# Attention with a spectral branch on one core: two diagonal row tiles share score columns, and the first loads, fills and projections are placed anew

## The chip, the cores and the metric

The kernel runs on one NeuronCore of a Trainium2 chip. The metric is the device time of one execution in microseconds (us), taken as the median of several executions. A profile of one execution shows every instruction of the five engines: TensorE (PE; its weight loads are shown apart as PEld), VectorE (DVE), ScalarE (ACT), GpSimd (POOL) and SyncE (SP, which here only issues DMAs).

## What is computed

The input x is 2 x 2048 x 256 (B = 2, S = 2048, D = 256). Cut to what matters, the reference is:

```
xn = layernorm(x)
q, k, v = xn @ wq, xn @ wk, xn @ wv      # 16 query heads, 4 key/value heads of 16
q, k = rope(q), rope(k)
scores = q k^T / 4, causal               # -inf above the diagonal
attn = softmax(scores) v
out = x + attn @ wo + real(ifft(fft(xn) @ w)) + bias
```

The spectral branch is linear, so the kernel turns its weights into one 256 x 256 matrix and multiplies with it.

## The kernel before, in words

**Tiles and stages.** The rows are cut into 8 blocks of 512 (`SB`), in the order (batch 0, j = 0), (batch 1, j = 0), (batch 0, j = 1) and so on, with j from 0 to 3. A block is 4 row tiles of 128 (`NI`). The 16 query heads are 4 groups of 4 heads, so there are 32 units (n, g) of a block and a group. All products of scores are made of bf16 parts: q and k are split in three parts each and stacked on 112 partitions (`qst`, `kst`), which gives scores of nearly float32 quality in one bf16 product. Most products are issued as four matmuls of 32 output partitions each (`product`, L151, with the matmul on L155), one for each quarter of the output partitions.

**Row maxima (kind A).** The softmax needs each row's maximum ahead of the exponentials. `maxima` (L593) makes slots for a unit: `row_max(i, k, pr)` handles row tile i of the block, key block k and two heads. PE writes both heads' scores into a pair of PSUM banks (`sm`, a ring of two such pairs) and DVE reduces them to one maximum for each row and head (L636, into `mx`). Where k is below j all 512 keys count. On the diagonal (k = j) row tile i sees (i + 1) x 128 keys, and each head takes eight matmuls: in each quarter q a mask product that writes -1e30 above the diagonal (L627, from column `at` to the end of the tile) and the scores added to it (L631). The lines are quoted here:

```python
for q in range(0, P, QD):
    to, at = ps[0][q : q + QD, e, :], wd - P + q
    nc.tensor.matmul(to[:, at:wd], ident_h[:, q : q + QD], mask[:, q:],
        start=True, stop=True, skip_group_check=True)
    nc.tensor.matmul(to[:, : at + QD], rows[:, q : q + QD], keys[:, : at + QD],
        start=False, stop=True, skip_group_check=True)
```

After the last slot of a unit `parts` (L644) combines the maxima over the key blocks and splits the negated maximum in three bf16 parts with seven small DVE reductions (L656); `spread` (L668) turns them onto partitions with four PE transposes, an ACT copy (`mt`) and a small DMA into `qst`, so that the next product subtracts the maximum by itself.

**Scores and values (kinds B and V).** `scores` (L693) makes the transposed scores of 128 keys for one head (`st`, three PSUM banks), and ACT takes the exponential (L745, or L747 two heads at once when no A is left). `values` (L767) multiplies them with V (L782). Groups are divided by their sums with DMAs and POOL, and `output` (L920) adds the output projection, the spectral product and x.

**Preparing a block.** `load_x` (L166) loads 512 rows with one DMA on SP. `row_stats`, `row_power` and `row_shift` (L233 to L252) make mean and inverse deviation on DVE and POOL. `project` (L379) normalizes (`norm`, L398), transposes (`transpose_x`, L405), multiplies with the weights (`features`, L419), rotates and splits. Block 0 does this on DVE, all later ones on POOL. `rotary_table` (L276) spreads the cosines and sines over columns (`expand`, eight DVE reductions, L293) and transposes them (`turn`). `ones` (L370) fills `va` and `kst` with ones. At the start PE runs 48 transposes of no use (L997) while the first loads are under way.

**The order.** A planner at the end of the kernel (L1127 on) writes the order of all instructions by hand. It keeps a clock for each engine from estimated costs (`use`, `send`, `through_bank`), takes at each step the piece that could start soonest, and looks up by when each A slot is due (`due`, L969 to L983, built from the `cols` that a slot states). The engines then work through this fixed order; changed costs or slot sizes move pieces everywhere.

Of the kernel before, what the change touches and what calls it, by code (L numbers as in the profile page):

```python
# [17 lines left out]
P = 128  # L18
# [5 lines left out]
def tile_attn_plus_spectral_ffn(  # L24
# [141 lines left out]
    def load_x(n):  # L166
        send("sp", 512, [slot("xt")], [("xt", "in", n)])
        take_slot("xt")
        xt[n] = work.tile([P, NI, D], F32, tag="xt", bufs=2, name=f"xt{n}")
        nc.sync.dma_start(out=xt[n], in_=block_rows(n))  # L170
# [41 lines left out]

    spec = {}
# [3 lines left out]
    def load_late():  # L217

        for name, src, tag, bufs in (
            ("wre", w_re, "inv", 2), ("dc", dft[0], "inv", 2),  # L220
            ("wim", w_im, "attT", 2), ("ds", dft[1], "avs", 3),
        ):
            take_slot(tag)
            spec[name] = work.tile([P, NK, D], F32, tag=tag, bufs=bufs, name=name)
            nc.gpsimd.dma_start(out=spec[name], in_=src.rearrange("(c p) n -> p c n", p=P))
            send("pool", 256, (), ["spec"])
        nc.gpsimd.dma_start(out=wo_sb, in_=wo.rearrange("(c p) n -> p c n", p=P))
        nc.gpsimd.dma_start(out=bias_sb, in_=bias.partition_broadcast(P))

# [3 lines left out]
    def row_stats(n, i):  # L233
        if i == 0:
            mv[n] = work.tile([P, NI, 2], F32, tag="mv", bufs=2, name=f"mv{n}")
        st = work.tile([P, 6], F32, tag="bn", bufs=3, name=f"bn{n}_{i}")
        nc.vector.bn_stats(st, xt[n][:, i, :])
        nc.vector.bn_aggr(mv[n][:, i, :], st)
        use("dve", 0.53, [("xt", "in", n)], [("mv", n)])

    def row_power(n):
        rstd[n] = work.tile([P, NI], F32, tag="rs", bufs=2, name=f"rs{n}")
        nc.gpsimd.tensor_scalar(rstd[n], mv[n][:, :, 1], EPS, None, ALU.add)
        nc.gpsimd.tensor_tensor(rstd[n], rstd[n], neg_half, ALU.pow)
        use("pool", 1.35, [("mv", n)], [("rs", n)])
# [30 lines left out]
    def rotary_table(j):  # L276
        ex = []

        def expand():
# [17 lines left out]
            use("dve", 1.15, at, [("trx", j)])  # L297
# [72 lines left out]
    def ones(n):  # L370
        e, eng, us = (nc.vector, "dve", 2.7) if n == 0 else (nc.gpsimd, "pool", 2.5)
        va[n] = const.tile([P, NI, NKV, QD], F32, tag=f"va{n}", name=f"va{n}")
        e.memset(va[n], 1.0)
        kst[n] = const.tile([P, NKV, SB], BF16, tag=f"kst{n}", name=f"kst{n}")
        for h in range(NKV):
            e.memset(kst[n][96:P, h, :], 1.0)
        use(eng, us, (), [("ones", n)])

    def project(n):  # L379
# [4 lines left out]
        MULT, SUB, CAST, NORM = (0.72, 0.72, 0.46, 0.33) if n == 0 else (1.23, 1.13, 0.63, 0.53)  # L384
        raw, sw, swp, part, ra, at = {}, {}, {}, {}, {}, {}
# [33 lines left out]
        def features(c):  # L419
            ps = bank(f"ps_q{n}_{c}")  # L420
            for k in range(NK):
                product(
                    ps, wp[:, k, c, :], xnT[n][:, k, :], start=(k == 0), stop=(k == NK - 1)
                )
# [3 lines left out]
            through_bank(  # L428
                1.83, ["wp", *(("xnT", n, k) for k in range(NK))], "act", 0.48, [("raw", "in", n, c)],
                [("raw", at[c] - ring["raw"])],  # L430
# [138 lines left out]
        for c in (NK, 0, 1):  # L569
            table = [("cs", j, 1)] * (n >= 2)  # L570
            pe.append(("pe", ["wp", *table, *xs], ["st", "raw"] + ["sw"] * (n >= 2), lambda c=c: features(c)))
# [21 lines left out]
    def maxima(n, g):  # L593
# [3 lines left out]

        def row_max(i, k, pr):

            wd = SB if k < j else (i + 1) * P  # L600
            ps, k_s = [], []

            def head(e):
                if e == 0:
                    k_s.append(take_slot("s"))
                    if not slots_done:
                        t["mx"] = work.tile(
                            [P, NI, NKV, NJ], F32, tag="mx", bufs=3, name=f"mx{n}_{g}"
                        )
                    slots_done.append(1)  # L610
                    ps.append(
                        ps_s.tile([P, 2, SB], F32, tag="s", name=f"sm{n}_{g}_{i}_{k}_{pr}")
                    )
                h = 2 * pr + e
                rows = qst[n, g][0:KC, h, i * P : (i + 1) * P]
                keys = kst[at_block[b, k]][0:KC, h, :]
                use(
                    "pe", (wd + 32 * (k == j)) * 4.28e-4 + (0.012 if k == j else 0.003),
                    [("stk", n, g), ("kst", at_block[b, k]), ("s", k_s[0] - ring["s"])],
                    [("pair", k_s[0])],  # L620
                )
                if k < j:
                    product(ps[0][:, e, :], rows, keys, True, True)
                else:
                    for q in range(0, P, QD):
                        to, at = ps[0][q : q + QD, e, :], wd - P + q
                        nc.tensor.matmul(  # L627
                            to[:, at:wd], ident_h[:, q : q + QD], mask[:, q:],
                            start=True, stop=True, skip_group_check=True,
                        )  # L630
                        nc.tensor.matmul(  # L631
                            to[:, : at + QD], rows[:, q : q + QD], keys[:, : at + QD],
                            start=False, stop=True, skip_group_check=True,
                        )
                if e == 1:
                    nc.vector.tensor_reduce(  # L636
                        t["mx"][:, i, 2 * pr : 2 * pr + 2, k], ps[0][:, :, :wd], AX.X, ALU.max
                    )
                    use("dve", 0.07 + 2 * wd / 960, [("pair", k_s[0])], [("s", k_s[0])])

            needs = [("stk", n, g), ("kst", at_block[b, k])]
            return lambda: head(0), lambda: head(1), 2 * wd + 150, needs

        def parts():  # L644

            top = t["mx"][:, :, :, : j + 1]
# [19 lines left out]
            use("dve", 1.35, (), [("np", n, g)])  # L666

        def spread():  # L668
            ps = bank(f"ps_m{n}_{g}", BF16)
            for i in range(NI):  # L670
                nc.tensor.transpose(
                    ps[0 : 3 * NKV, i * P : (i + 1) * P],
                    t["np"][:, i, :, :].rearrange("p a h -> p (a h)"),
                    ident_h,
# [7 lines left out]
        for i in range(NI):  # L682
            for k in range(j + 1):
                for pr in range(NKV // 2):
                    slots.append(row_max(i, k, pr))
# [170 lines left out]
    def divide(u):  # L856
# [3 lines left out]
        if g == 2:  # L860
            att[n] = work.tile([P, NI, 2, NKV, DH], F32, tag="att", bufs=1, name=f"att{n}")
# [142 lines left out]
    load_late()  # L1004
    row_shift(0)
    order_weights()

    def chain(n, starts, late=0):
# [3 lines left out]
        stats = [("dve", [("xt", "in", n)], [], lambda i=i: row_stats(n, i)) for i in range(NI)]  # L1012
# [5 lines left out]
        if n:  # L1018
            stream([("pool", [], [], lambda: ones(n))], s["ones"], s["stats"])
# [13 lines left out]
    def table(j, since):  # L1033
        expand, turn = rotary_table(j)
        last = [("cs used", at_block[B - 1, j - 2])] if j >= 2 else []
        stream(
            [("dve", last, ["raw", "raw2"], expand)]
# [248 lines left out]
```

## Time and profile before

| what | value |
|---|---|
| median of 3 runs | 926.1 us (925.84 to 926.69) |
| the profiled execution's own time | 926.6 us |
| its span in the profile | 924.9 us |
| mean granted PE clock | 0.995 |
| PE busy | 904.8 us (98%) |
| DVE busy | 749.3 us (81%) |
| ACT busy | 654.3 us (71%) |
| POOL busy | 370.2 us (40%) |

A busy PE counts each matmul from its start to a modelled end. Matmuls of different quarters and following matmuls overlap, so the busy time has the pipeline's latency in it, and idle time under the latency of one matmul is not seen; how fast PE really works is read from the distance between the starts of like groups. "issue" marks idle time that ended without any wait that the profile shows. The span is the time between first and last instruction; 1.7 us of the execution lie around it.

### The profile page before, as it was taken

To read this page: it belongs to the slowest core of one execution; us is meant where nothing else is said; L and a number is where in the kernel's file an instruction comes from. 1 tells how busy PE (TensorE), PEld (TensorE's weight loads), DVE (VectorE), ACT (ScalarE), POOL (GpSimd) and SP (SyncE) were. 2 spreads that over 40 slices of the span, in tenths; PEclk is the share of its full clock that TensorE was granted. 3 is DMA by queue.
4 is the path that set the end of the run, shared out by engine and by line. 5 is a ranking of instruction groups with operands and counts; after the bars stand their busy time and mean duration, and the time that the engine had idled before them with its cause. 6 is when DMAs were issued, how large, how long until landed. Compare 5 with 4: busy or idle time off the path is not lost.

```text
span 924.9 us, 39006 instructions
## 1 busy us (share of the span) xinstructions
PE 904.8 (98%) x17324; PEld 499.3 (54%) x17324; DVE 749.3 (81%) x1062; ACT 654.3 (71%) x1381; POOL 370.2 (40%) x556
## 2 busy tenths in 40 slices
PE   7999899999999999999999999999999999999997
PEld 4655565655555555555555555555455554645443
DVE  6878697789779997898995999979789989788601
ACT  3266665588757784888865777858687878588785
POOL 7287666824672414822246520311571021102121
PEclk9999999999999999999999999999999999999999
DMA  5435724351244011440002510010133001100000
GB/s 162 122 88 139 201 84 115 89 141 39 60 117 133 27 38 31 115 128 26 15 27 85 140 38 14 27 60 14 28 107 93 15 3 38 48 15 14 28 1 24
DMA packets 42024, 62.13 MB, mean 67 GB/s; under 512 B 8872, under 2 KB 32152, under 8 KB 41856
## 3 DMA queue, kind: packets, MB, share of 16 engines
q1 hardware_dynamic: 32432, 41.18, 16.7%
q0 software_dynamic: 8128, 17.69, 5.9%
q8 instruction: 135, 2.21, 1.0%
q10 hardware_dynamic: 1296, 0.79, 0.3%
q14 instruction: 33, 0.27, 0.1%
HBM read 32.75 MB, written 18.40 MB: 55 GB/s over the span
## 4 chain that ended last, share of the span: by engine, by line
PE 89%; DVE 4%; ACT 3%; issue 1%; DMA 1%; SPq 1%; POOL 1%; ACTq 0%; DVEq 0%; POOLq 0%
PE av L782 24%; PE st L155 22%; PE sm L155 17%; PE sm L631 7%; PE po L155 6%; PE ps_q L155 4%; DVE mx L636 2%; PE sp L155 2%; PE sm L627 2%; PE st L738 1%; ACT es L745 1%; PE ps_x L411 1%; PE st L734 1%; ACT es L747 1%; SPq L393 1%
## 5 line engine op out<-in xcount | busy, mean ns | idle before, releaser
L636 DVE TENSOR_REDUCE mx<-sm 128x2 f32<-128x1024 f32 (+3 forms) x640 | 649.1, 1058 | 87.7 <-PE sm L631 45.0
L745 ACT ACTIVATE es<-st 128x512 f32<-128x512 f32 (+3 forms) x1194 | 552.4, 543 | 179.7 <-PE st L155 145.5
L155 PE MATMUL st<-qst,kst 115*32 115x512 bf16 (+3 forms) x4264 | 327.1, 354 | 1.1 <-ACT es L745 0.4
L782 PE MATMUL av<-es,va 128*32 128x512 f32 (+3 forms) x2560 | 299.3, 530 | 0.8 <-issue 0.5
L155 PE MATMUL sm<-kst,qst 112*32 112x512 bf16 x3072 | 239.1, 379 | 0.1
L155 PEld LDWEIGHTS <-kst 115*32 115x32 bf16 x4608 | 160.8, 95 | 140.0 <-issue 64.1
L752 POOL TENSOR_SCALAR_AFFINE_SELECT es<-es 128x256 f32<-128x256 f32 x192 | 76.7, 407 | 274.9 <-ACT es L745 233.4
L155 PEld LDWEIGHTS <-qst 112*32 112x32 bf16 x3072 | 96.0, 96 | 93.0 <-issue 65.0
L631 PE MATMUL sm<-kst,qst 112*32 112x32 bf16 (+15 forms) x2048 | 122.0, 280 | 0.8 <-DMA qst<-part 0.8
L627 PE MATMUL sm<-mask,ident_h 128*32 128x64 bf16 (+3 forms) x2048 | 100.0, 201 | 1.2 <-DVE mx L636 0.9
L782 PEld LDWEIGHTS av<-es,va 128*32 128x32 f32 x2560 | 84.7, 109 | 28.3 <-ACT avs L796 2.6
L631 PEld LDWEIGHTS <-qst 112*32 112x32 bf16 x2048 | 66.1, 97 | 34.3 <-issue 20.7
L627 PEld LDWEIGHTS <-ident_h 128*32 128x32 bf16 x2048 | 66.0, 96 | 32.9 <-issue 26.0
L931 DVE TENSOR_TENSOR xr<-po,xr 128x256 f32<-128x256 f32 x36 | 15.3, 424 | 52.3 <-PE po L155 50.4
L817 POOL DMA_DIRECT2D res<-avs x30 | 18.2, 606 | 81.9 <-ACT avs L796 79.3
L155 PE MATMUL ps_q<-xnT,wp 128*32 128x512 f32 x384 | 45.5, 602 | 0.0
L747 ACT ACTIVATE es<-sp 128x1024 f32<-128x1024 f32 (+3 forms) x43 | 36.5, 907 | 7.3 <-PE sp L155 7.2
L427 ACT COPY raw<-ps_q 128x512 f32<-128x512 f32 x24 | 14.1, 586 | 35.1 <-PE ps_q L155 33.9
L518 POOL TENSOR_TENSOR ra<-raw,cs 128x512 f32<-128x512 f32 (+1 forms) x21 | 27.5, 1307 | 24.2 <-ACT raw L427 23.0
L738 PE MATMUL st<-qst,kst 115*32 115x160 bf16 (+15 forms) x512 | 36.4, 281 | 0.4 <-issue 0.4
L155 PE MATMUL po<-wo_sb,attT 128*32 128x256 f32 x512 | 35.0, 380 | 0.7 <-ACT attT L892 0.7
L734 PE MATMUL st<-mask_t,ident_h 128*32 128x128 bf16 (+3 forms) x512 | 30.6, 202 | 4.2 <-issue 3.3
(113 smaller groups left out, 663.0 us busy)
## 6 DMA issues: line engine op xcount, KB each, us to landing
qst<-run SPq DMA_DIRECT2D x62, 128.0 KB
res<-avs POOLq DMA_DIRECT2D x30, 256.0 KB, 2.9
run<-part SPq DMA_DIRECT2D x31, 192.0 KB
qst<-run SPq DMA_DIRECT2D x31, 192.0 KB
xt<-in_L_attn_x_dram SPq DMA_DIRECT2D x8, 512.0 KB
xr<-in_L_attn_x_dram SPq DMA_DIRECT2D x16, 256.0 KB
sw<-raw SPq DMA_DIRECT2D x60, 64.0 KB
attT<-res POOLq DMA_DIRECT2D x15, 256.0 KB, 4.2
```

The lines of the kernel that those rows point to most:

```text
L155: nc.tensor.matmul(to[q : q + QD], lhsT[:, q : q + QD], rhs, start=start, stop=stop)
L518: e.tensor_tensor(ra[c][:r], raw[c][:r], cs[j][:r, 0, :], ALU.mult)
L627: nc.tensor.matmul(to[:, at:wd], ident_h[:, q : q + QD], mask[:, q:], start=True, stop=True, skip_group_check=True,)
L631: nc.tensor.matmul(to[:, : at + QD], rows[:, q : q + QD], keys[:, : at + QD], start=False, stop=True, skip_group_check=True,)
L636: nc.vector.tensor_reduce(t["mx"][:, i, 2 * pr : 2 * pr + 2, k], ps[0][:, :, :wd], AX.X, ALU.max)
L734: nc.tensor.matmul(to[:, lo : at + QD], ident_h[:, q : q + QD], mask_t[:, : q + QD], start=True, stop=True, skip_group_check=True,)
L738: nc.tensor.matmul(to[:, at:], keys[:, q : q + QD], rows[:, at:], start=False, stop=True, skip_group_check=True,)
L745: nc.scalar.activation(es[u, t, pr][:, e, lo:], ps[:, lo:], AF.Exp, scale=SCALE)
L747: nc.scalar.activation(es[u, t, pr][:, :, lo:], wide[pr][:, :, lo:], AF.Exp, scale=SCALE)
L752: nc.gpsimd.affine_select(out=es[u, t, pr][:, :, lo : lo + P], in_=es[u, t, pr][:, :, lo : lo + P], pattern=[[0, 2], [1, P]], compare_op=A ...
L782: nc.tensor.matmul(av[u][QD * h : QD * (h + 1), lo:], va[at_block[b, t // NI]][:, t % NI, h, :], es[u, t, h // 2][:, h % 2, lo:], start=(t ...
L817: nc.gpsimd.dma_start(out=res[n, c][f], in_=avs[u])
```

## The change

Six things change together.

1. On the diagonal, row tiles 0 and 1 share the columns of one PSUM bank for each head (`first_rows`: 288 columns, two slots for a unit), and tiles 2 and 3 share 800 columns over two banks (`last_rows`: one slot for each head, four for a unit). In the odd tiles the four quarters of rows are taken in turned order, so that quarter q of the one tile needs as many columns more as quarter q of the other needs fewer. Mask products shrink to the 32 x 32 triangle on the diagonal.
2. DVE reduces these slots in groups of 32 columns into a table `top_g`. `parts` has three more small reductions: two add a constant table, which is zero or -1e30 by the row's quarter, to the groups whose owner depends on the quarter, and one takes the maximum over the groups of each tile.
3. `spread` uses matmuls in place of transposes, with a turned identity (`turned_h`) for the odd tiles.
4. The first block of x is loaded with four DMAs, and its statistics wait for their own quarter only. `turned_h` and `top_g` are filled at the start, on DVE and POOL.
5. The spreading of the first table stands between the first block's `row_power` and `row_shift`. The fills of block 1 wait for its normalization.
6. `features` is two pieces for the planner, one for each half of the contraction. Several planner costs are changed, and a late tile takes another buffer's place.

```diff
 def load_x(n):
...
+        step = NI if n else 1
+        for i in range(0, NI, step):
+            nc.sync.dma_start(out=xt[n][:, i : i + step, :], in_=block_rows(n)[:, i : i + step, :])
...
+    turned_h = const.tile([P, P], BF16, name="turned_h")
+    for q in range(0, P, QD):
+        nc.vector.tensor_copy(turned_h[:, q : q + QD], ident_h[:, P - QD - q : P - q])
...
+    G0, TE, TO, STEP = 10, 7, 35, 19
+    top_g = const.tile([P, 2, NKV, 3 * STEP], F32, name="top_g")
+    nc.vector.memset(top_g, NEG)
+    nc.vector.memset(top_g[:, :, :, 0:3], 0.0)
+    nc.vector.memset(top_g[:, :, :, 38:41], 0.0)
...
+        def rows_of(h, i, q):
+            at = i * P + (q if i % 2 == 0 else P - QD - q)
+            return qst[n, g][0:KC, h, at : at + QD]
...
+        def triangle(to, q, first):
+            add(to, ident_h[:, q : q + QD], mask[:, q : q + QD], first)
...
+        def first_rows(pr):
...
+                to = t["ps"][:, e, :]
+                for q in range(0, P, QD):
+                    triangle(to[q : q + QD, q : q + QD], q, True)
+                for q in range(0, P, QD):
+                    triangle(to[q : q + QD, 256:288], q, False)
+                for q in range(0, P, QD):
+                    add(to[q : q + QD, : q + QD], rows_of(h, 0, q), keys(h, 0, q + QD))
+                for q in range(0, P, QD):
+                    add(to[q : q + QD, q + QD : 288], rows_of(h, 1, q), keys(h, 0, 256 - q))
...
+        def last_rows(h):
...
+                    to = t["ps"][:, 1, :]
+                    for q in range(0, P, QD):
+                        triangle(to[q : q + QD, 384:416], q, True)
+                    for q in range(0, P, QD):
+                        add(to[q : q + QD, 0:416], rows_of(h, 3, q), keys(h, P - QD - q, SB - q))
...
+                to = t["ps"][:, 0, :]
+                for q in range(0, P, QD):
+                    triangle(to[q : q + QD, 384 + q : 416 + q], q, True)
+                for q in range(0, P, QD):
+                    add(to[q : q + QD, 128 : 416 + q], rows_of(h, 2, q), keys(h, 0, 288 + q))
+                for q in range(0, P - QD, QD):
+                    add(to[q : q + QD, 416 + q : SB], rows_of(h, 3, q), keys(h, 0, P - QD - q))
...
         def parts():
...
+            for lo, to in ((0, TE), (STEP, TO)):
+                both = rows[:, :, lo : lo + 2 * STEP].rearrange("p r (b c) -> p r c b", b=2)
+                nc.vector.tensor_reduce(rows[:, :, to : to + 3], both[:, :, 0:3, :], AX.X, ALU.add)
+            nc.vector.tensor_reduce(
+                t["mx"][:, :, :, :, j].rearrange("p e r h -> p e (r h)"),
+                rows[:, :, 3 : 3 + 2 * STEP].rearrange("p r (e c) -> p e r c", e=2)[:, :, :, 0:16],
+                AX.X, ALU.max,
+            )
...
     row_power(0)
     load_late()
+    table_0 = rotary_table(0)
+    table_0[0]()
     row_shift(0)
...
-            stream([("pool", [], [], lambda: ones(n))], s["ones"], s["stats"])
+            norm_1 = [("xn", 1, NI - 1)]
+            stream([("pool", norm_1, [], lambda: ones(n))], s["ones"], s["stats"])
```

## The prediction

> **What bounds the kernel now.** I read the page's busy times, then the chain of waits, then windows of stages, then the starts of single groups.
>
> ```profile
> PE 904.8 (98%) x17324; PEld 499.3 (54%) x17324; DVE 749.3 (81%) x1062; ACT 654.3 (71%) x1381; POOL 370.2 (40%) x556
> PE 89%; DVE 4%; ACT 3%; issue 1%; DMA 1%; SPq 1%; POOL 1%; ACTq 0%; DVEq 0%; POOLq 0%
> ```
>
> PE sets the time: it is on 89% of the chain. PE work taken off shortens the run wherever PE itself is full. The windows say where that is:
>
> ```profile
> 80.00:100.00 20.00, 18.54 (x616) 12.01 (x607) 15.80 (x33) 13.58 (x37) 14.54 (x17) 1.00 0.60 157
> 100.00:120.00 20.00, 16.16 (x507) 11.51 (x506) 13.94 (x29) 12.04 (x34) 15.33 (x23) 0.91 0.75 195
> 400.00:500.00 100.00, 99.84 (x1820) 53.53 (x1815) 83.16 (x116) 72.96 (x156) 29.63 (x50) 1.00 0.17 52
> ```
>
> The columns after the stretch and its length are PE, PEld, DVE, ACT, POOL, clock. From 400 to 500 us PE never stops and DVE has 17% to spare. From 80 to 120 us (end of the j = 0 units) no engine is full: they wait for each other. So a PE saving counts fully for the 24 units with j > 0, and in part for the 8 with j = 0.
>
> **Part 1: the diagonal products on PE.** What does such a head cost PE today? The distance of the starts says it. Tile 0 (160 columns in each quarter, 128 of them in the first mask), then tile 3 (544):
>
> ```profile
> 161.09 0.22 PE L627 MATMUL sm<-mask,ident_h 128*32 128x128 bf16 x4
> 161.14 0.22 PE L631 MATMUL sm<-kst,qst 112*32 112x96 bf16 x4
> 161.18 0.22 PE L627 MATMUL sm<-mask,ident_h 128*32 128x128 bf16 x4
> 161.22 0.22 PE L631 MATMUL sm<-kst,qst 112*32 112x96 bf16 x4
> 161.26 0.40 PE L155 MATMUL st<-qst,kst 115*32 115x512 bf16 x4
> ...
> 179.26 0.22 PE L627 MATMUL sm<-mask,ident_h 128*32 128x128 bf16 x4
> 179.31 0.38 PE L631 MATMUL sm<-kst,qst 112*32 112x480 bf16 x4
> 179.50 0.22 PE L627 MATMUL sm<-mask,ident_h 128*32 128x128 bf16 x4
> 179.54 0.39 PE L631 MATMUL sm<-kst,qst 112*32 112x480 bf16 x4
> 179.74 0.41 PE L155 MATMUL st<-qst,kst 115*32 115x512 bf16 x4
> ```
>
> The 0.22 us are latency. The pitch of a head is (161.26 - 161.09) / 2 = 85 ns for tile 0 and 240 ns for tile 3; the same reading gives 125 ns for tile 1 (167.16 to 167.41) and 185 ns for tile 2 (173.63 to 174.00). Sum for a head: 635 ns. Two heads of plain 512-column products take 0.43 us (702.05 to 702.48), which is 0.42 ns a column. By that the four tiles' columns alone would take 67, 121, 175 and 228 ns: each head has 4 to 18 ns more, about 5 ns for each of the two matmuls in a quarter, and most where one has only 32 columns. In tile 0's first quarter 128 columns take 54 + 5 ns, so its 32-column matmul takes the other 26 to 29 ns, not the 13 of its columns.
>
> The change removes, for each head, 1408 - (352 + 448 + 416) = 192 columns in each quarter, and adds 3 matmuls (35 for 32) of which many have 32 columns: two masks in each quarter of `first_rows`, one in each piece of `last_rows`. Two prices:
> - By columns: 192 x 0.42 = 81 ns a head, less the extra matmuls' 5 ns: 10 us for 128 heads of 32 units. The trace's 32-column pitch contradicts it.
> - The Trainium skill ("TensorE: Matmul & The Clock Gate", section "Wait — 56ns, not 53.3ns?") says that start-to-start never drops below about 25 ns however few the columns. This rule speaks against the change, which trades long masks for short ones. The trace has 28 ns by my reading. With 28 ns for each 32-column matmul and 0.42 ns a column + 5 ns otherwise, `first_rows` takes 180 to 196 ns by quarter (mean 187), `last_rows` 206 and 199: 592 ns. Before, by the same formula: 638, which the 635 measured confirm.
>
> I take 46 ns a head, times 128: **-5.9 us**. Ends: -3 (the slowest quarter of each group counts, 611 ns) and -10 (columns). Some 1.5 us of it lies in the j = 0 units, where it counts in part; I leave it in, since the early stage has gains below that I price low.
>
> **Part 2: DVE.** The forms of L636 give its price:
>
> ```profile
> L636 DVE TENSOR_REDUCE mx<-sm 128x2 f32<-128x1024 f32 x448 | 526.6, 1218 | 56.8 <-PE sm L155 35.8 <-PE sm L631 17.6 <-PE st L155 0.6
> L636 DVE TENSOR_REDUCE mx<-sm 128x2 f32<-128x256 f32 x64 | 25.9, 419 | 10.2 <-PE sm L631 9.1
> ```
>
> The slope is (1218 - 419) / 768 = 1.04 ns an element, on 153 ns. Diagonal slots before: 2 x (419 + 685 + 952 + 1218) = 6.55 us a unit. After: two of 576 elements (752 ns) and four of 800 (985 ns), 5.44 us, and in `parts` two reductions of 48 elements (near L656's 170 to 190 ns) and one of 256 (about 420): 0.8 us. Together -0.3 us a unit, 10 us over the run, on an engine with spare time: I cost it at nothing. The 0.8 us also makes the maximum's chain longer (`parts`, `spread`, `mt`, first scores). What hides it is the planner's lead of 3 to 5 score steps of about 1.8 us each; without cover it costs 0.8 x 32 = 25 us, so a lead that fails in a few units costs 1 to 3 us. `spread`'s matmuls have the transposes' columns and stay at L671's price.
>
> **Part 3: the start.**
>
> ```profile
> 5.19 0.43 DVE L237 BATCH_NORM_STATS2 bn<-xt 128x6 f32<-128x256 f32 x1 [0.56 <-DMA xt<-in_L_attn_x_dram]
> ...
> 8.93 0.16 DVE L249 SCALAR_TENSOR_TENSOR sh<-mv,rs 128x4 f32<-128x4 f32 x1 [1.51 <-POOL rs L244]
> 9.01 1.63 DVE L293 TENSOR_REDUCE trx<-trig 128x128 f32<-128x128 f32 x8
> ...
> 10.55 1.89 DVE L399 TENSOR_SCALAR xt<-xt,rs,sh 128x256 f32<-128x256 f32 x4
> ```
>
> DVE waits 0.56 us for x. The quarter loads remove that wait, but the new fills stand ahead of the statistics: four casts of 32 columns (0.4 to 0.6 us, by L208's two 64-column copies in 0.29), 456 elements of `top_g` (0.43, by `va`'s 512 in 0.48), two small fills (0.2): 1.1 us. So the statistics start at about 5.75 and end at 7.95, 0.5 later than now; the split load gains nothing. Then the table (1.63 us) fills DVE's 1.51 us wait for POOL, and the normalization starts at 9.8 in place of 10.55: **-0.75 us**. SP's three more issues (0.5 us each) push the table's load and block 1's back 1.5 us; the table's must land by 7.95, and the first loads are all over by about 8: up to +0.5. POOL's two selections on `top_g` lie in its idle time before 7.5.
>
> PE's useless transposes end at 8.66 and its next work starts at 10.30; in 12 to 15 us the clock is at 0.50. With the gap 1 us shorter the dip may go: between 0 and -1.2 us, I take -0.4.
>
> On POOL's timeline block 1's `rs` (L243) starts only at 18.47, behind the fills of blocks 1 and 2, and later POOL idles: 11.1 us before the next `rs` (33.84), 5.4 us before `ra` (44.87), then it runs without a gap from 48.7 to 80.7. After the change block 1's `rs` follows POOL's six DMA issues, its transposes stand on PE ahead of the spectral products, and POOL can begin its rotation near 27 us in place of 45. PE has no less to do by that; it only starves less at 80 to 120 us. Between 0 and -6 us, near 0 since those windows' waits are mutual: **-2 us**. The split of `features` adds no instruction; where A slots go in between it holds one of three banks longer, 0 to +3 us, I take 0. The late tile's new place was last read near 31 us and is written near 886: nothing.
>
> **Sum:** -5.9 - 0.75 - 0.4 - 2 = -9 us, on the profiled execution's 926.6 (924.9 of span and 1.7 around it): 917.6. The median shown is 0.5 lower: **917 us**.
>
> **Rivals.**
> 1. *The early stage closes up* (17%). 80 to 120 us has 5.3 us without any PE work and 1.7 us lost to a half clock. If the earlier rotation removes that, another 5 us go: 912. Against it: ACT and DVE also stand at 60 to 79% there.
> 2. *The price of short matmuls eats the gain* (14%). Only 24 units count, at 24 ns: -2.3, and -0.75 at the start: 923. For it: 384 more matmul and load pairs.
> 3. *Late instructions, and slower* (11%).
>
> ```profile
> 108.00 0.28 PE L734 MATMUL st<-mask_t,ident_h 128*32 128x128 bf16 x4 [2.92 <-issue]
> ```
>
> PE's program comes in 135 packets of 2.21 MB (the page's q8). The one for this place started only at 105.2, while the DMA engines were full, and PE stood for 2.92 us and then ran 3.4 us at half clock: 4.6 us in all. The Trainium skill ("Runtime: NRT & Kernel Launch", section "Instruction fetch mechanics") holds that fetching in 16 KiB blocks is hidden, which would cost the change's 768 more instructions nothing; this row says otherwise when DMAs crowd. Denser short instructions and transfers moved forward into 50 to 100 us could make such stalls frequent. Two more of them eat the gain, three give 931: slower. Against it: one in 135 today; and today's may vanish as well.
> 4. *As forecast* (58%).
>
> **Range and chances.** Part 1's ends (3 to 10 us), the early stage (0 to 8) and rival 2 give 911.5 to 924, which leaves out rival 3 and the best of rival 1. A measurement tells 0.2% (1.9 us) from no change. Rivals 1 and 4 and most of 2 are faster: 0.85; 0.05 within; 0.10 slower.
>
> **What would show it.** The pitch of a `first_rows` head near 187 ns and of a `last_rows` head near 405; DVE's reductions at 752 and 985 ns; the first normalization near 9.8 us; POOL's first rotation near 27; no new rows of 2 us and more with "issue" on PE. Wrong would be: pitches as before, `mt` later than its unit's first score, or several such stalls.

## The result, and the profile after

The changed kernel takes 920.33 us (median of 12 runs, 918.32 to 923.77); the kernel before took 925.41 us beside it (12 runs, 922.52 to 930.26). The ratio is 0.9951, with a 95% interval of 0.9936 to 0.9966: faster by 0.49%, about 4.5 us (the medians are 5.1 apart). The forecast of 917 us stood for a ratio of 0.990. The sign was right and the time lies in the range, but the gain is about half of the sum of -9 us, and the interval excludes that sum. The profiled execution took 919.05 us, with a span of 917.3 us.

The page of the changed kernel, the same rows as before (busy times, then the packets and megabytes that brought PE's instructions, then the chain of waits):

```profile
PE 891.7 (97%) x17708; PEld 485.7 (53%) x17708; DVE 742.6 (81%) x1101; ACT 655.9 (72%) x1378; POOL 373.0 (41%) x558
...
q8 instruction: 138, 2.26, 1.0%
...
PE 89%; DVE 4%; ACT 4%; issue 3%; ACTq 0%; POOL 0%; DMA 0%; SPq 0%; POOLq 0%; DVEq 0%
```

PE still sets the time. What is new on the chain is "issue": 3% where it was 1%, while DMA and SP's queue have left it. The program needs three more packets of instructions. The windows of the stages (stretch, length, PE, PEld, DVE, ACT, POOL, clock, DMA share, GB/s; the last row is of a second profile of the same kernel, taken with run 10 below):

```profile
80.00:100.00 20.00, 15.39 (x597) 11.11 (x586) 15.24 (x34) 13.70 (x36) 14.02 (x17) 1.00 0.55 152
100.00:120.00 20.00, 17.01 (x594) 12.62 (x598) 16.01 (x34) 13.85 (x36) 12.95 (x20) 1.00 0.60 163
400.00:500.00 100.00, 100.00 (x1889) 53.14 (x1884) 84.76 (x121) 73.38 (x156) 29.91 (x51) 1.00 0.11 35
```

```profile
95.00:100.00 5.00, 4.89 (x151) 3.55 (x154) 2.84 (x4) 2.27 (x7) 2.51 (x4) 0.66 0.52 150
```

From 400 to 500 us PE has no idle time at all, so there the saved PE work counts in full. From 80 to 100 us PE is busy for 15.39 us where it was for 18.54, with about as many matmuls begun (597 for 616): the end of the j = 0 units still starves PE. In this profile the clock is not the reason, since the half clock of before (0.91 from 100 to 120 us) is gone. It is not gone for good: the second profile has 3.4 us of it from 95.5 us on (0.66 over the window of 5 us).

**The diagonal.** PE's timeline around one slot of `last_rows` (start, duration, line, tiles):

```profile
309.66 0.63 PE L155 MATMUL st<-qst,kst 115*32 115x512 bf16 x5
310.11 0.20 PE L677 MATMUL sd<-mask,ident_h 128*32 128x32 bf16 x4
310.14 0.36 PE L677 MATMUL sd<-kst,qst 112*32 112x416 bf16 x4
310.32 0.20 PE L677 MATMUL sd<-mask,ident_h 128*32 128x32 bf16 x4
310.34 0.34 PE L677 MATMUL sd<-kst,qst 112*32 112x288 bf16 x6
310.51 0.38 PE L155 MATMUL st<-qst,kst 115*32 115x512 bf16 x1
```

From 310.11 to 310.51 a head takes 400 ns (forecast 405: 206 and 199), and a group of four 32-column masks, one for each quarter, takes 30 ns of it (310.11 to 310.14). Two heads of `first_rows` start 180 ns apart (100.65 and 100.83; forecast 187). So a head costs 580 to 590 ns in place of 635. DVE's groups by form (busy us, mean ns):

```profile
L652 DVE TENSOR_REDUCE top_g<-sd 128x25 f32<-128x800 f32 x128 | 121.0, 983 | 32.1 <-PE sd L677 27.0 <-PE st L855 3.4 <-PE st L155 0.7
L652 DVE TENSOR_REDUCE top_g<-sd 128x18 f32<-128x576 f32 x64 | 46.8, 749 | 9.9 <-PE sd L677 9.7
L754 DVE TENSOR_REDUCE mx<-top_g 128x16 f32<-128x256 f32 x32 | 13.5, 423 | 1.1
L753 DVE TENSOR_REDUCE top_g<-top_g 128x24 f32<-128x48 f32 x64 | 10.7, 209 | 1.1
```

Forecast were 985, 752, about 420 and 170 to 190 ns.

**The start.** DVE's timeline:

```profile
5.73 0.43 DVE L264 BATCH_NORM_STATS2 bn<-xt 128x6 f32<-128x256 f32 x1
...
7.88 1.60 DVE L320 TENSOR_REDUCE trx<-trig 128x128 f32<-128x128 f32 x8
9.47 0.16 DVE L276 SCALAR_TENSOR_TENSOR sh<-mv,rs 128x4 f32<-128x4 f32 x1
9.67 1.58 DVE L426 TENSOR_SCALAR xt<-xt,rs,sh 128x256 f32<-128x256 f32 x4
```

The statistics start at 5.73 (forecast 5.75), the table fills the wait for POOL, the normalization comes at 9.67 (forecast 9.8, before 10.55). PE's first projection starts at 12.31 in place of 13.76, the half clock of 12 to 15 us is gone, and POOL rotates block 1 from 26.97 (forecast near 27).

**What is new.** The longest entries of PE's waits that ended for no reason that the profile shows (us in total, times, longest):

```profile
PE sd L677 <- issue: 4.7, 4, 1.8
PE st L855 <- issue: 3.4, 3, 1.3
...
PE av L899 <- issue: 1.5, 1, 1.5
```

Before, the same view had 3.3 us on the score masks (two, one of them the 2.92 us row of the prediction) and 0.9 us besides: 4.2 us in all, against 9.6 here. Two of the new ones in the timeline, inside `sd` slots of the j = 0 units, and the longest one of the second profile:

```profile
95.48 0.19 PE L677 MATMUL sd<-mask,ident_h 128*32 128x32 bf16 x2 [1.81 <-issue]
...
100.03 0.20 PE L677 MATMUL sd<-mask,ident_h 128*32 128x32 bf16 x3 [1.49 <-issue]
```

```profile
95.11 0.19 PE L677 MATMUL sd<-mask,ident_h 128*32 128x32 bf16 x2 [2.91 <-issue]
```

PE stops in the middle of a group of four masks, which nothing in the program asks for; a pause of PE is called a stand below. I laid every gap of PE longer than 0.2 us against the 16 KiB packets of the instruction queue, and call a packet "beside" a gap when it is under way in it or ended less than 0.5 us before it. In this profile six gaps of 1.0 us and more have one; the packet starts 1.1 to 1.6 us before PE stands, and PE goes on about 1.4 us after the packet has ended. From 35 to 135 us the gaps with a packet sum to 2.9 us before and to 8.3 us after; in the second profile they sum to 6.2 us, of which 1.2 ended on a wait for ACT. That is rival 3's mechanism: six stands of 1.0 to 1.8 us in this profile in place of one of 2.9, and one of 2.9 us with a half clock behind it in the second.

### The profile page after: what moved, and what is told of

It is laid out like the page before. It is cut to its first block, busy times and chain, and to the rows that moved or that the text cites. A ratio compares the mean times of both kernels' runs of the same rounds, so it can differ in the third digit from the quotient of the medians.

```text
span 917.3 us, 39844 instructions
## 1 busy us (share of the span) xinstructions
PE 891.7 (97%) x17708; PEld 485.7 (53%) x17708; DVE 742.6 (81%) x1101; ACT 655.9 (72%) x1378; POOL 373.0 (41%) x558
## 4 chain that ended last, share of the span: by engine, by line
PE 89%; DVE 4%; ACT 4%; issue 3%; ACTq 0%; POOL 0%; DMA 0%; SPq 0%; POOLq 0%; DVEq 0%
PE av L899 25%; PE st L155 22%; PE sm L665 17%; PE sd L677 8%; PE po L155 6%; PE ps_q L155 4%; ACT es L862 2%; PE sp L155 2%; PE st L855 1%; ACT es L864 1%; PE st L851 1%; PE ps_x L438 1%; PE ps_m L785 0%; PE ps_ff L155 0%; DVE mx L652 0%
## 5 line engine op out<-in xcount | busy, mean ns | idle before, releaser
L652 DVE TENSOR_REDUCE mx<-sm 128x2 f32<-128x1024 f32 x384 | 450.2, 1217 | 42.2 <-PE sm L665 38.7
L652 DVE TENSOR_REDUCE top_g<-sd 128x25 f32<-128x800 f32 (+1 forms) x192 | 167.8, 905 | 42.0 <-PE sd L677 36.7
L665 PEld LDWEIGHTS <-qst 112*32 112x32 bf16 x3072 | 93.1, 96 | 90.9 <-issue 58.8
L677 PE MATMUL sd<-kst,qst 112*32 112x416 bf16 (+12 forms) x2432 | 101.9, 259 | 1.1 <-issue 1.0
L677 PE MATMUL sd<-mask,ident_h 128*32 128x32 bf16 x2048 | 79.4, 179 | 5.6 <-issue 3.7
L677 PEld LDWEIGHTS <-ident_h 128*32 128x32 bf16 x2048 | 60.0, 95 | 35.6 <-issue 26.8
L677 PEld LDWEIGHTS <-qst 112*32 112x32 bf16 x2432 | 52.9, 95 | 19.1 <-issue 8.8
L864 ACT ACTIVATE es<-sp 128x1024 f32<-128x1024 f32 (+3 forms) x46 | 39.3, 915 | 8.0 <-PE sp L155 7.8
L855 PE MATMUL st<-qst,kst 115*32 115x512 bf16 (+15 forms) x512 | 35.4, 279 | 3.4 <-issue 3.4
```

Source lines behind the costliest of these rows:

```text
L652: nc.vector.tensor_reduce(out, of, AX.X, ALU.max)
L665: nc.tensor.matmul(t["ps"][q : q + QD, e, :], rows_of(h, i, q), kst[at_block[b, k]][0:KC, h, :], start=True, stop=True,)
L677: nc.tensor.matmul(to, lhsT, rhs, start=first, stop=True, skip_group_check=True)
L855: nc.tensor.matmul(to[:, at:], keys[:, q : q + QD], rows[:, at:], start=False, stop=True, skip_group_check=True,)
L864: nc.scalar.activation(es[u, t, pr][:, :, lo:], wide[pr][:, :, lo:], AF.Exp, scale=SCALE)
```

## The experiments

"After" below is the changed kernel. Differences to it are differences of the two ratios to the kernel before, times 925 us, since not all kernels were timed beside the same runs of before. By the two intervals, such a difference is known to about 2 to 2.5 us.

**1 and 2. Each half of the change alone.** The first is the changed kernel with `maxima` (and so `parts` and `spread`) of before; the second is the kernel before with the new `maxima`, its fills and the late tile's place.

```diff
 # first: the changed kernel, in maxima
-        def first_rows(pr):
-        def last_rows(h):
+            wd = SB if k < j else (i + 1) * P
 # second: the kernel before, and
+    turned_h = const.tile([P, P], BF16, name="turned_h")
+    top_g = const.tile([P, 2, NKV, 3 * STEP], F32, name="top_g")
+        def first_rows(pr):
+        def last_rows(h):
```

> The changed kernel with the row maxima of before: the new start, table, fills, first loads and pieces of projections alone. Theory (the packing brings about 6 us, the start's 1.5 us are lost again in the j = 0 units): within 1 us of the kernel before, 924 to 926, with the first spread about 1.5 us earlier than before. Rival (the start and the early stage bring half or more, the packing little): 2 to 4 us faster than before, 921 to 923.

> The kernel before with the packed diagonal slots, their fills and the maxima's three reductions alone. Theory (PE work sets the time): 5 to 6 us faster than before, 919 to 920, as the whole change. Rival (the j = 0 units give back): 2 to 3 us faster, 922 to 923.

Measured: the start alone 922.99 us, ratio 0.9975 [0.9956, 0.9994], so -2.3 us (-4.1 to -0.6) where the sum had -3.15. The diagonal alone 922.53 us, ratio 0.9966 [0.9949, 0.9983], so -3.1 us (-4.7 to -1.6) where the sum had -5.9. The two add up to -5.4; both together gave -4.5 (-5.9 to -3.1). So these intervals show no sign that the parts hinder each other. The start's interval holds its sum, the diagonal's does not: the missing microseconds are mostly the diagonal's.

Where does the diagonal lose them? I summed PE's work instruction by instruction with the prediction's prices (0.42 ns a column and 5 ns, 28 ns for 32 columns, four times the columns for a float32 product) and took this work off the start of each unit's `spread` in the trace. What is left is how far PE has fallen behind its own work by then, in us, in one execution of each kernel:

| kernel | PE work in all | behind at unit 0 | unit 6 | unit 8 | unit 31 | end |
|---|---|---|---|---|---|---|
| before | 867.1 | 11.8 | 18.7 | 25.7 | 46.3 | 57.8 |
| after | 861.3 | 10.2 | 21.9 | 25.6 | 43.9 | 56.0 |
| start alone | 867.1 | 10.1 | 18.4 | 23.1 | 41.4 | 53.0 |
| diagonal alone | 861.3 | 12.4 | 24.5 | 29.9 | 49.5 | 61.6 |

(The first j > 0 unit is unit 8; the prices are a model, so only differences between kernels count.) The packed diagonal takes 5.8 us of work away in both kernels that have it, as priced. Against the kernel of the same start without it, PE falls behind by 3.5 us more (after against start alone) or 5.8 us more (diagonal alone against before) by unit 6. At unit 8 it is 2.5 and 4.2 us, and from there to the end hardly more is lost: 30.4 us against 29.9, and 31.7 against 32.1. The second profile of the changed kernel, worked out in the same way, is 2.7 us further behind than the start alone at unit 6 and 2.4 at unit 8, but loses 1.5 us more from there to the end. So most of the loss sits in the j = 0 stage.

PE's waits that end in "issue" from 35 to 135 us follow the packing: 1.0 us with the start alone, 4.2 before, 9.2 with the diagonal alone, 9.6 and 5.7 in the two profiles of after.

**3 and 4. Every 32-column mask doubled**, once for j > 0 alone (384 more groups of four on PE) and once for j = 0 alone (128 more groups). A second -1e30 on a masked key leaves it masked, and the order is that of the changed kernel.

```diff
         def triangle(to, q, first):
             add(to, ident_h[:, q : q + QD], mask[:, q : q + QD], first)
+            if j > 0:      # the other kernel: if j == 0
+                add(to, ident_h[:, q : q + QD], mask[:, q : q + QD], False)
```

> The changed kernel with each 32 x 32 mask product issued twice in the units with j > 0, at the same place in the order: 96 heads, four 32-column matmuls more in each quarter. Theory (28 ns for each, as read from the pitch): 96 x 4 x 28 = 10.8 us slower than the changed kernel, about 931. Rival (by columns and 5 ns a matmul, 18 ns): 6.9 us slower, about 927; by columns alone (13 ns): 5.1 us, about 925.

> The same doubling in the 8 units with j = 0 alone: 32 heads, 1024 more PE instructions, which are four more 16 KiB pages. Theory (in the j = 0 units PE stands because pages of instructions come too slowly for short matmuls): each page costs one more stand of 1 to 2.8 us beside its work, 6 to 11 us slower than the changed kernel, 926 to 931, with more and longer rows of issue on PE between 35 and 130 us. Rival (these units wait for DVE, ACT and POOL): at most the work of 32 x 4 x 28 ns = 3.6 us, less where it falls into waits: 920 to 924.

Measured for j > 0: 929.91 us, ratio 1.0044 [1.0024, 1.0064], 8.6 us more than after: 22 ns for each group (about 16 to 28 by the intervals), between the 13 ns of its columns and the 28 ns of the prediction. Measured for j = 0: 932.34 us, ratio 1.0068 [1.0046, 1.0090], 10.8 us more, for a third of the work: 3.6 us at 28 ns. PE's waits in this kernel:

```profile
PE sd L677 <- issue: 9.7, 7, 2.6
PE st L853 <- issue: 3.0, 1, 3.0
...
PE st L857 <- issue: 2.2, 2, 1.4
```

With a last row of 0.2 us, PE's waits for "issue" are 15.1 us, against 9.6 after; the gaps with an instruction packet beside them sum to 13.2 us from 35 to 135 us, against 8.3. So in the j = 0 stage an added PE instruction costs about three times its time, and a good part of the extra is time in which PE waits for its program. In the j > 0 stage it costs its own time and little more (one stand of 1.83 us with "issue" and a packet beside it, at 289 us, is in its profile).

**What the clock adds.** A long stand seems to have a second price. Between 35 and 135 us the profiles of all kernels here have eight stands of PE of 2.5 us and more, and each has a stretch of 3.4 us at half the clock, which begins between 0.5 us before the end of the stand and 1.3 us after it. Of 38 stands of 1.0 to 2.2 us two have one. Such a stretch costs up to 1.7 us. Run 4's profile has three of them (from 92.3, 102.6 and 123.0 us; its granted clock is 0.95 from 35 to 135 us), which is up to 5 us of its extra time. The first profile of after and the start alone have none there, before, the diagonal alone and the second profile of after one each.

The granted clock, averaged over each kernel's executions, points the same way: 0.9949 in run 4, 0.9952 with the diagonal alone, 0.9966 after, 0.9977 before, 0.9982 with the start alone. For the diagonal alone against before that is, as an estimate, up to 0.0024 x 923 = 2.2 us of lost clock. The two profiles in the table have as many such stretches as each other, so what the table shows as lost is not the clock; over all executions the clock may be a large part of it.

**5 and 6. Fewer, wider masks.** The triangles that lie in the same columns for all four quarters are written by one matmul with 128 output partitions in place of four with 32: 1536 PE instructions less in all, or 384 less where this is done for j = 0 alone.

```diff
-                for q in range(0, P, QD):
-                    triangle(to[q : q + QD, 256:288], q, False)
+                add(to[:, 256:288], ident_h, tri_all)
...
-                    for q in range(0, P, QD):
-                        triangle(to[q : q + QD, 384:416], q, True)
+                    add(to[:, 384:416], ident_h, tri_all, True)
```

> The changed kernel with the triangles that all four quarters write to the same columns made by one full-width matmul in place of four: two for each head, 1536 PE instructions less in all (6 pages). Theory (late pages): the stands with a page in the j = 0 units shrink from 8.3 us to 3 to 5 us, and if a full-width matmul costs PE no more than the four, the time falls by 3 to 5 us to 915 to 917. Rival (a full-width matmul makes the four quarters wait for each other, by up to half of a head's skew of 50 ns): 256 x 50 ns = 13 us more work at most, half of it likely: 920 to 926.

> The same in the units with j = 0 alone: 384 PE instructions less where pages come late. Theory (late pages): 2 to 4 us faster than the changed kernel, 916 to 918, with shorter stands between 35 and 130 us. Rival (the stands come from the order, not from the count of instructions): within 1 us of the changed kernel, 919 to 921.

Measured everywhere: 953.7 us, ratio 1.0314 [1.0298, 1.0330], 34 us more than after, or 131 ns for each of the 256 wide masks. PE's timeline shows where:

```profile
321.34 0.61 PE L155 MATMUL st<-qst,kst 115*32 115x512 bf16 x8
321.88 0.19 PE L681 MATMUL sd<-tri_all,ident_h 128*128 128x32 bf16 x1
322.00 0.36 PE L681 MATMUL sd<-kst,qst 112*32 112x416 bf16 x4
322.19 0.19 PE L681 MATMUL sd<-mask,ident_h 128*32 128x32 bf16 x4
```

The wide mask takes 120 ns to the next start (the four small ones took 30), and the two heads of scores ahead of it take 540 ns to their successor where 430 is the rule: about 0.1 us going in and 0.1 us coming out. The Trainium skill ("TensorEngine Tiling (Array Packing)", section "Key Properties") states that a change of the tiling mode drains TensorE, without a size; this trace agrees, with about 0.1 us each way. The run as a whole lost 131 ns for each wide mask and not 200; what makes up for the rest is not shown. In the j = 0 stage alone: 924.09 us, ratio 0.9981 [0.9966, 0.9996], 2.8 us more than after (0.7 to 4.8), though its 64 wide masks cost 8.4 us by the run's 131 ns. The gaps with a packet fell from 8.3 to 2.6 us. The numbers fit (8.4 - 5.7 = 2.7), and within that interval they also fit the second profile's 6.2: some of what the longer work costs seems to come back as shorter stands. It is no gain.

**7 and 11. Holding POOL's early rotation.** In the changed profile DVE's last pieces of block 0 are slow just when POOL starts to rotate block 1 (DVE's timeline of after, then PE's):

```profile
27.34 1.38 DVE L571 CAST part<-raw 128x512 bf16<-128x512 f32 x1
28.75 0.69 DVE L577 TENSOR_TENSOR rb<-raw,part 128x512 f32<-128x512 f32 x1
29.48 1.38 DVE L580 CAST part<-rb 128x512 bf16<-128x512 f32 x1
30.90 1.67 DVE L585 TENSOR_TENSOR part<-rb,part 128x512 bf16<-128x512 f32 x1
```

```profile
34.88 0.20 PE L677 MATMUL sd<-mask,ident_h 128*32 128x32 bf16 x4 [1.86 <-DVE top_g L652]
```

The casts took 0.43 us in the profile before and the last subtraction 0.69, and PE's gap of 1.86 us follows. The first attempt gave the planner one condition more:

```diff
-                (eng, [("raw", "in", n, c), ("cs", j, 0)], [], lambda c=c: rotate(c, 0)),
+                (eng, [("raw", "in", n, c), ("cs", j, 0)] + [("part", "in", 0, 1, "l")] * (n == 1 and c == NK),
+                 [], lambda c=c: rotate(c, 0)),
```

> The changed kernel with block 1's first rotation on POOL held until DVE has split block 0's last part, so that the two engines don't work at once there. Theory (DVE's operations of 27 to 33 us, up to 1.67 us in place of 0.69, are slowed by POOL beside them, and PE's 1.86 us before the second slot of unit 0 come from it): those operations fall back to 0.43 to 0.69 us, the 1.86 us go, and the run is up to 2 us faster or the same, since block 1 is 6 us later: 918 to 921. Rival (they are slow by themselves or by a DMA): durations as in the changed kernel.

Measured: 921.62 us, ratio 0.9959 [0.9942, 0.9976]. It was no test: a condition of the planner moves the order of issue, and POOL, with nothing else ahead of it, started the rotation at 26.98 us as before. The second attempt keeps that condition and makes POOL itself wait, by reading one element of DVE's last result:

```diff
+                if n == 1 and c == NK:
+                    nc.gpsimd.tensor_copy(hold, last_l[0, 1][:, 2, 0:1])
                 ra[c] = work.tile([P, SB], F32, tag=f"ra{min(n, 1)}", bufs=1, name=f"ra{n}_{c}")
```

> The run that asked the planner to hold block 1's rotation left POOL's first rotation at 26.98 us, so it held nothing. Here POOL copies one element of the last part that DVE makes of block 0 before it rotates: the order on every engine is that run's, and only the start of POOL's rotation moves. Theory (DVE's slow copies at 27 to 33 us come from POOL running beside it): DVE's casts at 27.3 and 29.5 take 0.43 us in place of 1.38, its last subtraction 0.69 in place of 1.68, DVE is ready 2.9 us earlier, and PE's gap of 1.9 us at 33 to 35 us goes. If that gap counts at the end: 919.5 to 920.5. Rival: POOL's rotation now starts near 29 us and ends some 2 us later, the early stage absorbs both, and the time stays within 1 us of that run's 921.6.

Measured: 920.92 us, ratio 0.9952 [0.9934, 0.9971]. DVE's timeline in this kernel:

```profile
27.33 0.43 DVE L575 CAST part<-raw 128x512 bf16<-128x512 f32 x1
...
28.52 0.43 DVE L584 CAST part<-rb 128x512 bf16<-128x512 f32 x1
28.98 0.69 DVE L589 TENSOR_TENSOR part<-rb,part 128x512 bf16<-128x512 f32 x1
```

So POOL's rotation was the cause: without it beside them the same three operations take 1.55 us in place of 4.43, and PE's gap is gone. And yet the time stays. The windows say why, first after, then this kernel:

```profile
10.00:35.00 25.00, 21.23 (x275) 8.61 (x277) 22.10 (x42) 8.50 (x17) 22.70 (x32) 1.00 0.52 152
35.00:80.00 45.00, 42.31 (x1229) 27.81 (x1224) 32.47 (x79) 23.39 (x56) 32.78 (x37) 1.00 0.49 123
```

```profile
10.00:35.00 25.00, 22.49 (x313) 9.44 (x312) 21.13 (x46) 8.51 (x17) 20.96 (x33) 1.00 0.48 144
35.00:80.00 45.00, 41.11 (x1187) 27.42 (x1186) 30.89 (x76) 23.42 (x56) 33.52 (x38) 1.00 0.49 127
```

PE is busy 1.26 us longer by 35 us and 1.20 us less from there to 80 us. From 10 to 80 us it has begun 1500 matmuls (313 + 1187) against 1504. So the early gain is gone before the j = 0 stage is over. (Later this profile also has a stand of 2.91 us and a half clock from 97.0 us on.)

**8 and 9. The planner's costs.** The changed kernel plans with other costs than before. The first kernel gives it all of the old ones back, the second only the old cost of `parts`.

```diff
-            use("dve", 2.0, (), [("np", n, g)])
+            use("dve", 1.35, (), [("np", n, g)])
```

> The changed kernel with the planner's cost constants of before: the same pieces in another order. It shows how much a mere reordering moves. If order alone moves the early stage, the time differs from the changed kernel's by 1 to 3 us either way; if not, by under 1 us: 919.5 to 921.

> The changed kernel with one planner cost put back: 1.35 us in place of 2.0 for the small reductions at a unit's end, which really take 1.9 us now. Theory (the run with all old costs lost 16 us mainly because PE came to the spread of the maxima before DVE had them): PE waits for them again, and most of the 16 us return, 928 to 936. Rival (another of the old costs did it): within 2 us of the changed kernel, 918 to 922.

Measured: 936.07 us, ratio 1.0125 [1.0096, 1.0153] with all old constants, 16 us more than after; 932.23 us, ratio 1.0076 [1.0063, 1.0088] with that of `parts` alone, 13 us more than after beside it. PE's weight loads of `spread` that wait for `parts`, first in the second kernel, then after:

```profile
PEld L785 <- DVE np L769: 19.9, 28, 1.2
```

```profile
PEld L785 <- DVE np L769: 7.1, 18, 0.6
```

A planner that believes `parts` to be as short as before puts `spread` too early in PE's order, and PE then stands in front of it, 28 times and for longer. The waits grew by 12.8 us, which is about what the run lost. This is the cover that Part 2 priced at 25 us, and this one number in the source holds half of it. (The added 0.65 us of belief is near the 0.8 us that `parts` became longer.)

**10. The packing for j > 0 alone**, with the long slots of before in the j = 0 stage, and the changed kernel again beside it.

```diff
+    def maxima(n, g):
+        return (maxima_packed if blocks[n][1] else maxima_long)(n, g)
```

> The changed kernel with the packed slots in the units with j > 0 alone; j = 0 has the diagonal slots of before, with 24 PE instructions less for each unit. Theory (in the j = 0 units late pages take more than the packing saves): the stands with a page fall from 8.3 to 3 us or less there, the 24 other units keep their 24 x 4 x 46 ns = 4.4 us: 2 to 4 us faster than the changed kernel, 916 to 918. Rival (the j = 0 packing is worth its 1.5 us and the stands are the order's): 1 us slower than the changed kernel or the same, 920 to 922.

> The changed kernel once more, beside the two others on the same chip. Every theory expects the ratio of its first comparison, 0.9936 to 0.9966, about 920.

Measured: 920.79 us, ratio 0.9951 [0.9938, 0.9963]; the changed kernel beside it 919.56 us, ratio 0.9932 [0.9912, 0.9952]. The stands did go: gaps with an instruction packet fell to 2.2 us (8.3 and 6.2 in the two profiles of after), and PE is 19.3 us behind at unit 6 in place of 21.9. But by unit 8 it is 26.3 behind, as much as after. PE's waits in this kernel name others in their place:

```profile
PE st L950 <- issue: 2.4, 4, 0.9
PE st L954 <- issue: 2.2, 3, 1.2
PE sm L657 <- DVE mx L666: 2.2, 4, 1.3
```

There is also a half clock at 117.9 us, 3.4 us long, which is up to 1.7 us of what was lost again. So the forecast of a gain from giving PE fewer, longer instructions in that stage fell. The `spread` of unit 8, near the end of the stage, starts at 134.7 us before, 132.8 after, 132.2 with the start alone, 136.5 with the diagonal alone and 135.3 here, in no order that follows what PE has saved; PE work put on top does move it (148.3 us in run 4). What else holds that time, the late instructions, the clock, ACT, DVE or the transfers, these runs do not settle; no version beat the changed kernel.

## Why the prediction was right, and where it was not

- **What bounds the kernel: right.** PE is full for j > 0 (100.00 us of 100), and mutual waits rule from 80 to 120 us.
- **Part 1, the price of a head: right.** 400 and 180 ns against 405 and 187. By these prices PE's whole work fell by 5.8 us. (With the stated prices the two sums come to 598 and 644 ns, not 592 and 638; their difference is the same 46.) The floor of about 25 ns, which was weighed there, lies between the 22 ns of the doubled masks and the 30 ns of the timeline, as the price of a group of four; inside a group the starts are closer.
- **Part 1, the sum: here it failed.** "Some 1.5 us of it lies in the j = 0 units, where it counts in part; I leave it in": the diagonal alone brought -3.1 us (-4.7 to -1.6), not -5.9. The j = 0 stage brought nothing and took some more. At unit 8 PE is 2.5 and 4.2 us further behind its work than without the packing: about 2 us of that is work saved by then that bought no time, and 0.6 and 1.8 us are a later start of that unit's `spread` (132.8 for 132.2, 136.5 for 134.7). The saving from unit 8 on was kept, for the most part.
- **Rival 3, the size of it: also wrong.** "One in 135 today" made late instructions an event of 4.6 us with a chance of 11%. They came in both profiles of the changed kernel (8.3 and 6.2 us) and with the diagonal alone (7.3), and belonged into the sum as a cost of the early stage. The row of 2.92 us in the profile of before was the sign. The Trainium skill's statement ("Runtime: NRT & Kernel Launch", section "Instruction fetch mechanics") that fetching is mostly hidden holds in the changed kernel for j > 0 (no stand of over 0.4 us there has a packet beside it) and not for j = 0. The sign named as proof against the forecast, a new row of 2 us with "issue", is missing in the first profile, where the longest is 1.81, and stands in the second: 2.91 us and then 3.4 us at half clock, as in the row of before. With this stand in it the execution took 919.78 us, no more than the others.
- **Part 2: right but for a remainder.** DVE's durations are as forecast, and the lead of the planner covers most of the longer `parts`; with the old constant 13 us were lost, where 25 was the bound. The cover is not whole: after 135 us the weight loads of `spread` wait 6.8 us for `parts`, against 2.4 before and 3.6 with the start alone. What this cost is not shown; against the start alone, the table and the second profile leave 0.5 to 1.5 us for it.
- **Part 3: right in its steps, and in size within the interval.** 9.67 us, no half clock, POOL at 26.97; -2.3 us (-4.1 to -0.6) for -3.15. The -2 us for the early rotation cannot be told apart within it. That rotation also slowed DVE beside it by 2.9 us, which the prediction did not see and which costs nothing that run 11 could measure.
- **Rival 2** (923 us) has -2.3 us for the diagonal, which lies in the measured interval, but for reasons of which only one holds: that the 24 units with j > 0 alone count. Its 24 ns a head do not: the heads cost what the sum said. **Rival 1** did not come: the early stage did not close up.

The step that failed is thus the diagonal's term of the sum: -5.9 in the sum, -3.1 measured. That the time lies in the range is in part luck: the range was drawn wide for other terms, and the cost of late instructions was left out of it. That late instructions are part of the difference is supported by their stands, which come and go with the packing, and by run 4. How large a part is open: run 10 removed most of them and gained nothing, and the half clocks, which the prediction has only in rival 3 and at the start, were not varied by themselves.

## What to carry to other kernels

A saving counts where the engine is full in the windows. In the stage of mutual waits it counted as nothing here, and instructions that came on top had a price of their own: 128 groups of small matmuls cost 10.8 us for 3.6 us of work. One profile is one execution: the second one of the same kernel showed a stand and a half clock that the first did not have. When a hand-written order is planned from stated costs, change the cost together with the code: one constant left at its old value cost 13 us here. And a condition in a planner is not a wait on the engine; look up the start in the trace before a test is believed.

## What the runs showed of the hardware

- **PE waits for its own program.** Instructions come in packets of 16 KiB, about 257 of PE's recorded instructions each (35416 over 138 packets; the 3072 more of the doubled masks for j > 0 brought 12 more packets). Where PE ran through short matmuls and the DMA engines were half busy (0.55 to 0.60 from 80 to 120 us), a packet began only 1.1 to 1.6 us before PE ran out, and PE went on about 1.4 us after it had landed. In the stands of 2.5 us and more of all profiles it began about when PE ran out, or up to 0.9 us later.
- **A stand of 2.5 us or more went with 3.4 us at half clock** in eight of eight cases between 35 and 135 us; one of 1.0 to 2.2 us in two of 38.
- **A change between 32 and 128 output partitions costs about 0.1 us in each direction** between column-tiled bf16 products (from the timeline; over the whole run 131 ns for each wide mask, net of the four small ones that it replaces).
- **DVE and POOL hold each other up.** While POOL ran operations that read two tiles, DVE's float32 to bf16 casts took 1.38 us for 0.43, and a subtraction of two tiles took 1.67 for 0.69. A subtraction that DVE began at 28.75 us, 0.03 us ahead of POOL's next operation, kept its 0.69, and POOL's took 1.79 us where it took 1.27 in run 11. The statistics right after them (0.42 and 0.18 us, with POOL busy until 34.3) were not slowed. This agrees with the Trainium skill ("SBUF — State Buffer", section "Who interferes with whom"): a cast can be blocked by POOL for a whole instruction, an operation with two inputs in SBUF contends with POOL's reads, and one with a single input does neither outside of the modes with two ports.
